# One transformer block on one core: the SBUF addresses of the MLP's matmul operands, and of one attention buffer, are moved by 64 or 192 bytes

## The chip, the cores and the metric

The kernel runs on one core of a Trainium2 chip. The metric is the device time of one execution in microseconds (us); lower is better. Three runs of the kernel before took 735.03, 736.0 and 736.13 us, median 736.0. A fourth execution was profiled: 735.27 us, of which the profile's span covers 733.4 us.

## The reference

A PixArt-style block: self-attention, cross-attention to a context, and an MLP, for 16 batches of 256 tokens with 256 features, 16 heads, and an MLP of 1024 hidden features, all in float32.

```python
x_norm = modulate(_ln(x), shift_a, scale_a)
q, k, v = jnp.split(x_norm @ W_qkv + b_qkv, 3, axis=-1)
...
x = x + gate_a[:, None] * (attn_out @ W_proj + b_proj)
q_c = _ln(x) @ W_qc + b_qc
k_c, v_c = jnp.split(_ln(context) @ W_kvc + b_kvc, 2, axis=-1)
...
x = x + (c_attn_out @ W_cproj + b_cproj)
x_norm2 = modulate(_ln(x), shift_m, scale_m)
h = jax.nn.gelu(x_norm2 @ W_mlp1 + b_mlp1)
x = x + gate_m[:, None] * (h @ W_mlp2 + b_mlp2)
```

## The kernel before

**Number format.** A matrix product is made of three float32r matmuls: each operand is split into a high part and a low part, and high·high, high·low and low·high are added in PSUM (`mm3` at L461 and `mm3_tok` at L470). The names carry it: `hh` and `hl` are the high and low parts of the hidden values, `xTh` and `xTl` those of a transposed input, `h_q` and `l_q` those of a query.

**A matmul and its operands.** Each matmul has stationary weights (128 columns, read by a weight load, `PEld` in the profile) and moving rows (256 columns, streamed by the matmul itself, `PE`). The weight load of the next matmul runs while the rows of the present one are streamed. Every 128x128x256 matmul of this kernel has a weight load of its own.

**Attention, the first 550 us.** There are 32 units (16 of self-, 16 of cross-attention). Unit n holds its queries and keys in `big[n % 3]` (L85), three buffers of 16 KB in each partition, and its values in `vts[n % 3]`. In each beat of a unit PE makes scores `s` of the next unit (for the row maxima) and transposed scores `st` of this one, both with weights and moving rows from a `big` buffer. The exponentials go to `pt` tiles (4 KB, five buffers, `exp` at L782), which are the moving rows of `o` (`av_part`, L805), four column groups of 32 with weights from `vts`. Between them stand projections of other units, with 64 rows each, in two halves of the array side by side. Their weights and rows come from `wself`, `wcross` (the resident weight tiles) and `xTh`/`xTl`.

**MLP, from 553 us on.** The 16 batches are cut in 4 chunks of 256 hidden features, 64 chunks in all. Each chunk has a first product of 12 matmuls (`mlp_first`, L920; weights `W1` = `wself`, moving rows the normalised input, which stands in the no longer used `wcross`; its PSUM tile is `ph`), a gelu on ACT (`mlp_gelu`, L953) that writes `hf` and `hh`, a subtraction on POOL that writes `hl`, and a second product of 12 matmuls (`mlp_second`, L974; weights `hh` and `hl`, moving rows `W2` = `big[2]`; PSUM tile `st` or `s`). The loop at L1274 puts the first product of chunk i+2 ahead of the second product of chunk i-1, so that PE alternates: 12 matmuls `ph`, 12 matmuls `st` or `s`, and so on. The first six batches have their input transposed by four PE transposes (`mlp_T`, L869, PSUM tile `psT_m`, moving rows `ident`); the others by DVE and DMA.

**Order and places.** Every engine's order is the program's order (`InOrder`, L40; all its instructions have line L51 in the profile). Tiles get their SBUF address in the order in which they and their tags first appear, so one tile's size moves all that follow. The kernel before already has one such shift: `ROWS` (L133) puts the MLP's input 48 elements (192 bytes) into a slot of `wcross`.

```python
ROWS = [cross(1 - i, 48) for i in range(2)]
homes = (("pt", 5), ("qkh", 3), ("qkl", 3))
W2 = [big[2][:, 0], big[2][:, 1]]
```

**Places within 256 bytes.** The built program gives each tile's byte address in its partition. Its remainder by 256 is, before: `wself` and `wcross` 32; `ROWS` 224; `big` 160, all three; `vts` 160; `hh`, `hl` and the other tiles of the tags `qkh` and `qkl` 224; `pt` 224; `xTh`, `xTl`, `xn`, `A`, `oT` 224; `ident` 128. The `homes` are the tags of `hf`, `hh` and `hl`. A matmul's slices start at multiples of 512 bytes in these tiles, except for `vts`, whose heads lie 128 bytes apart (160 and 32 in turn).

Of the kernel before, what the change touches and what calls it, by code (L numbers as in the profile page):

```python
# [10 lines left out]
F32 = mybir.dt.float32  # L11
F32R = mybir.dt.float32r
# [4 lines left out]
P = 128  # L17
# [4 lines left out]
def pixart_block(  # L22
# [8 lines left out]
    B, N, H = x.shape  # L31
# [3 lines left out]
    NT = N // P  # L35
# [24 lines left out]
    const = ctx.enter_context(tc.tile_pool(name="const", bufs=1))  # L60
    work = ctx.enter_context(tc.tile_pool(name="work", bufs=2))
# [20 lines left out]
    mhalf = const.tile([P, 2], F32, name="mhalf")  # L82
    POOL.memset(mhalf, -0.5)

    big = [const.tile([P, 2, 8, N], F32R, name=f"big{i}") for i in range(3)]  # L85
    vts = [const.tile([P, NT, NH, 32], F32, name=f"v{i}") for i in range(3)]
    mxs = [const.tile([P, 160], F32, name=f"mx{i}") for i in range(3)]
    for t_ in mxs:
# [5 lines left out]

    BMOD, BQKV, BKVC, BM1 = 0, 12, 20, 24
    BQ, BK, BQC, BKC = 32, 34, 36, 38
    ct_ = work.tile([B, 2, H], F32, tag="qkh", name="c_sb", bufs=3)
    c_sb, th = ct_[:, 0], ct_[:, 1]
    SP.dma_start(c_sb, cond)
    X = {}  # L100

# [66 lines left out]

    ts = [work.tile([P, 2, KC, H], F32, tag="pt", name=f"wf{i}", bufs=5) for i in range(3)]
    wm0, wm1, wk, wq, wv = (ts[i // 2][:, i % 2] for i in range(5))  # L170
    dummy = const.tile([P, 2], F32, name="dummy")

    def f_load():
        X[0] = work.tile([P, NT, H], F32, tag="x", name="x_0", bufs=5)
# [152 lines left out]
    def layernorm(src, name):  # L327

        o = Box()

        def stats():
            o.st = work.tile([P, NT, 6], F32, tag="bnst", name=f"st_{name}")
            for t in range(NT):
                DVE.bn_stats(o.st[:, t], src()[:, t])

        def rstd(power=True):
            o.mv = work.tile([P, NT, 2], F32, tag="bnmv", name=f"mv_{name}")
            for t in range(NT):
                DVE.bn_aggr(o.mv[:, t], o.st[:, t])
            o.rs = work.tile([P, NT], F32, tag="rstd", name=f"rs_{name}")  # L340
            if power:
                o.pow()

        def pow():
            POOL.tensor_scalar(o.rs, o.mv[:, :, 1], EPS, None, ALU.add)
            POOL.tensor_tensor(o.rs, o.rs, mhalf, ALU.pow)

        def apply(eng=E_['LN'].get(name[0])):
            o.xn = work.tile([P, NT, H], F32, tag="xn", name=f"xn_{name}", bufs=3)
            for t in range(NT):  # L350
                if eng == "act":
                    ACT.activation(o.xn[:, t], src()[:, t], AF.Identity, bias=o.nb[:, t:t + 1],
                                   scale=o.rs[:, t:t + 1])
                else:
                    (DVE if eng == "dve" else POOL).tensor_scalar(
                        o.xn[:, t], src()[:, t], o.mv[:, t, 0:1], o.rs[:, t:t + 1],
                        ALU.subtract, ALU.mult)

        def shift():
            o.nb = work.tile([P, NT], F32, tag="nb", name=f"nb_{name}")  # L360
            POOL.tensor_scalar(o.nb, o.mv[:, :, 0], -1.0, None, ALU.mult)
            POOL.tensor_tensor(o.nb, o.nb, o.rs, ALU.mult)

        o.steps, o.pow, o.shift = [stats, rstd, apply], pow, shift
        return o

# [672 lines left out]
    for n, v in (("0", u0), ("1", u1), ("2", u2)):  # L1039
        for c in "KQV":  # L1040
            o = getattr(v, c)
# [8 lines left out]
    for n, v in (("0", u0), ("1", u1), ("2", u2)):  # L1050
        word["T" + n + "t"], word["T" + n + "h"], word["T" + n + "l"] = v.T[0].parts
        word["T" + n + "p"] = v.T[0].low_pool
        for c in "KQ":
            o = getattr(v, c)
# [206 lines left out]
    last, o, q = units[-1], units[-1].post, units[-2].post  # L1261
# [97 lines left out]
```

## Time and profile before

| | |
|---|---|
| three runs | 735.03, 736.0, 736.13 us, median 736.0 |
| the profiled execution | 735.27 us, its span 733.4 us |
| busy in the span | PE 99%, PEld 87%, DVE 79%, ACT 76%, POOL 74% |
| TensorE clock granted | 1.00 in nearly all of the span |
| DMA | 35.7% of 16 engines on SP's queue |

The profile lists for each engine how long its instructions ran. PE and PEld are two records of one engine: the matmuls, and the weight loads that overlap them. Matmuls overlap each other too, since one is recorded until its last row has left the array, so the distance between the starts of two matmuls says more of the pace than their durations. The timeline view joins equal neighbours into one row: start of the first, time in which they ran, name, and their count after an x. In the `x12` rows the distance to the start of the row behind is the time of 12 matmuls.

### The profile page before, as it was taken

What the parts mean: (1) busy time and instruction counts of PE and PEld (TensorE: products, weight loads), DVE (VectorE), ACT (ScalarE), POOL (GpSimd) and SP (SyncE); (2) the same over time, 40 slices, a digit from 0 to 9 for tenths busy, and PEclk for the clock granted to TensorE, in tenths of its full rate; (3) what the DMA queues carried; (4) which work ended last, traced back from release to release, by engine and by line L of the source; (5) the groups of instructions that cost most, each with busy time, mean ns of one, the idle gap of its engine ahead of it and who ended that gap; (6) DMA issues with size and microseconds to landing.
All of it is one profiled execution on the core that took longest, in us unless ns stands there. A gap on an engine that the chain in (4) does not pass through costs nothing.

```text
span 733.4 us, 24916 instructions
## 1 busy us (share of the span) xinstructions
PE 725.7 (99%) x10112; PEld 640.9 (87%) x10112; DVE 582.1 (79%) x1218; ACT 556.2 (76%) x961; POOL 545.7 (74%) x574
## 2 busy tenths in 40 slices
PE   9999999999999999999999999999999999999997
PEld 9788888888888888888888888888888999999997
DVE  4878888889888888988888989888745676686772
ACT  4368898888888888888888888899886666666653
POOL 6877578869687786968678898889646767767743
PEclk9999999999999999999999999999999999999999
DMA  6654434433434343343434344344221313334321
GB/s 191 208 163 144 146 121 132 145 109 114 155 127 144 127 151 121 116 147 126 152 120 159 126 161 146 139 148 147 81 60 44 117 59 101 89 98 103 85 62 57
DMA packets 67109, 90.56 MB, mean 123 GB/s; under 512 B 6194, under 2 KB 38740, under 8 KB 66996
## 3 DMA queue, kind: packets, MB, share of 16 engines
q1 hardware_dynamic: 66164, 86.88, 35.7%
q8 instruction: 80, 1.31, 0.7%
q0 software_dynamic: 560, 1.84, 0.7%
q14 instruction: 33, 0.27, 0.1%
q10 hardware_dynamic: 272, 0.26, 0.1%
HBM read 26.97 MB, written 8.46 MB: 48 GB/s over the span
## 4 chain that ended last, share of the span: by engine, by line
PE 95%; DVE 2%; POOL 1%; issue 1%; ACT 1%; POOLq 0%; ACTq 0%
PE s L51 19%; PE o L51 16%; PE st L51 16%; PE ph L51 10%; PE ps_q L51 4%; PE ps_qc L51 4%; PE ps_kc L51 4%; PE ps_v_c L51 3%; PE ps_k L51 3%; PE ps_v_s L51 3%; PE ps_P_s L51 3%; PE ps_P_c L51 2%; PE ps_h L51 1%; PE psT_q L51 1%; PE psA_c L51 1%; PE psA_s L51 1%
## 5 line engine op out<-in xcount | busy, mean ns | idle before, releaser
L51 DVE TENSOR_REDUCE mx<-s 128x2 f32<-128x512 f32 x504 | 324.5, 684 | 64.1 <-PE s L51 57.0
L51 ACT ACTIVATE pt<-st 128x1024 f32<-128x1024 f32 x252 | 259.1, 1028 | 17.6 <-PE st L51 10.6
L51 PE MATMUL s<-big 63*128 63x256 f32 (+1 forms) x1024 | 186.2, 299 | 0.5 <-DVE mx L51 0.2
L51 PEld LDWEIGHTS s<-big 63*128 63x128 f32 (+1 forms) x1024 | 133.5, 186 | 19.9 <-DVE l_kc L51 6.6
L51 PE MATMUL st<-big 64*128 64x256 f32 (+1 forms) x1024 | 134.1, 297 | 0.0
L51 POOL TENSOR_TENSOR hl<-hf,hh 128x512 fp32r<-128x512 f32 x64 | 85.4, 1338 | 53.7 <-ACT hh L51 53.4
L51 PE MATMUL o<-pt,v 128*32 128x256 f32 x2048 | 123.8, 382 | 0.0
L51 PEld LDWEIGHTS st<-big 64*128 64x128 f32 (+1 forms) x1024 | 96.5, 186 | 14.6 <-issue 12.8
L51 PEld LDWEIGHTS o<-pt,v 128*32 128x32 f32 x2048 | 60.0, 109 | 41.5
L51 PE MATMUL ph<-wcross,wself 128*128 128x256 f32 x672 | 88.1, 281 | 0.0
L51 PEld LDWEIGHTS ph<-wcross,wself 128*128 128x128 f32 x672 | 82.8, 189 | 0.0
L51 ACT ACTIVATE hf<-ph,bT 128x256 f32<-128x256 f32 x114 | 48.0, 473 | 32.6 <-PE ph L51 32.6
L51 ACT ACTIVATE hh<-ph,bT 128x256 fp32r<-128x256 f32 x114 | 47.9, 472 | 25.9 <-PE s L51 13.5
L51 ACT COPY oT<-o 128x512 f32<-128x512 f32 x63 | 37.0, 587 | 33.0 <-PE o L51 33.0
L51 PE MATMUL ps_kc<-xTh_c,wcross 64*128 64x256 f32 x256 | 46.7, 292 | 0.0
L51 PE MATMUL st<-big,hh 128*128 128x256 f32 x256 | 45.8, 279 | 0.0
L51 PE MATMUL s<-big,hh 128*128 128x256 f32 x256 | 45.7, 278 | 0.0
L51 PE MATMUL ps_v_c<-wcross,xTh_c 64*128 64x256 f32 x256 | 44.2, 292 | 0.0
L51 PE MATMUL ps_k<-xTh_s,wself 64*128 64x256 f32 (+1 forms) x232 | 43.6, 294 | 0.0
L51 PE MATMUL ps_qc<-xTh_q,wcross 64*128 64x256 f32 x256 | 41.5, 282 | 0.0
L51 PE MATMUL ps_q<-xTh_s,wself 64*128 64x256 f32 (+1 forms) x240 | 40.7, 287 | 0.0
L51 POOL TENSOR_SCALAR xn_c<-c,mv_c,rs_c 128x256 f32<-128x256 f32 x32 | 39.0, 1228 | 1.7
(236 smaller groups left out, 2154.8 us busy)
## 6 DMA issues: line engine op xcount, KB each, us to landing
big<-h_kc SPq DMA_DIRECT2D x32, 256.0 KB
big<-h_qc SPq DMA_DIRECT2D x32, 256.0 KB
big<-h_k SPq DMA_DIRECT2D x30, 256.0 KB
big<-h_q SPq DMA_DIRECT2D x29, 256.0 KB
g<-gd SPq DMA_DIRECT2D x16, 256.0 KB
c<-in_ctx_dram SPq DMA_DIRECT2D x16, 256.0 KB
big<-l_kc SPq DMA_DIRECT2D x16, 256.0 KB
big<-l_qc SPq DMA_DIRECT2D x16, 256.0 KB
```

The source lines that it names most:

```text
L51: i = f(*a, **k)
```

## The change

Nothing is computed otherwise, and no instruction is added, removed or moved: on all five engines the instructions of the two built programs stand in the same order, with the same shapes and as many waits. (Two read or write `th` in a buffer of its own, which was the second half of `c_sb`.) What differs is where tiles lie. `big[2]` becomes 256 bytes larger and its view starts 64 bytes in. The tag `qkl` is first used early (by `th`), so its buffers now lie behind those of `qkh`. `dummy` grows from 8 to 96 bytes, which moves all behind it, and the tag `bnst` has five small buffers in place of two, which brings the tiles behind it back to their old remainder.

```diff
-    big = [const.tile([P, 2, 8, N], F32R, name=f"big{i}") for i in range(3)]
+    big = [const.tile([P, 16 * N + 64 * (i // 2)], F32R, name=f"big{i}") for i in range(3)]
+    big = [t[:, 16 * (i // 2):16 * (i // 2) + 16 * N].rearrange("p (a k n) -> p a k n", a=2, k=8)
+           for i, t in enumerate(big)]
...
-    ct_ = work.tile([B, 2, H], F32, tag="qkh", name="c_sb", bufs=3)
-    c_sb, th = ct_[:, 0], ct_[:, 1]
+    c_sb, th = [work.tile([B, 2, H], F32, tag=t, name=n, bufs=3)[:, 0] for t, n in (("qkh", "c_sb"), ("qkl", "th"))]
...
-    dummy = const.tile([P, 2], F32, name="dummy")
+    dummy = const.tile([P, 24], F32, name="dummy")[:, :2]
...
-            o.st = work.tile([P, NT, 6], F32, tag="bnst", name=f"st_{name}")
+            o.st = work.tile([P, NT, 6], F32, tag="bnst", name=f"st_{name}", bufs=5)
```

Call the **step** from one matmul to the next the address of the first one's moving rows less that of the next one's weights, by remainder of 256. By the built programs:

| tile | remainder before | now |
|---|---|---|
| `big[2]` (`W2`; queries and keys of every third unit) | 160 | 224 |
| `hh`, `hl` (tags `qkh`, `qkl`) | 224 | 32 |
| `pt` | 224 | 32 |
| `wself`, `wcross`, `ROWS`, `big[0]`, `big[1]`, `vts`, `xTh`, `xTl`, `xn`, `A`, `oT`, `ident` | as above | unchanged |

| from matmul to matmul | step before | now |
|---|---|---|
| within 12 `ph` | 192 | 192 |
| within 12 `st` or `s` of the MLP | 192 | 192 (0 in one run, whose `hh` and `hl` lie in `xTh` and `xTl`) |
| from `ph` to `st` or `s` of the MLP | 0 | 192 |
| from `st` or `s` of the MLP to `ph` | 128 | 192 |
| from the transposes `psT_m` to `ph` | 96 | 96 |
| within `s` or `st` of attention | 0 | 0 |
| between `s` and `st` of two units, one of them in `big[2]` | 0 | 64 or 192 |
| within `o` | 64 and 192 | 128 and 0 |

## The prediction

> **What bounds the kernel now.** I read the busy shares and the chain of waits first, then busy time by stage. The first columns of the stage rows are the stretch, its length, and PE's busy time with its matmuls.
>
> ```profile
> PE 725.7 (99%) x10112; PEld 640.9 (87%) x10112; DVE 582.1 (79%) x1218; ACT 556.2 (76%) x961; POOL 545.7 (74%) x574
> PE 95%; DVE 2%; POOL 1%; issue 1%; ACT 1%; POOLq 0%; ACTq 0%
> 200.00:360.00 160.00, 159.91 (x2632) 135.82 (x2628) 139.31 (x299) 135.22 (x210) 121.70 (x130) 1.00 0.38 135
> 660.00:724.00 64.00, 64.00 (x552) 64.00 (x551) 41.85 (x77) 38.42 (x93) 40.12 (x36) 1.00 0.31 80
> ```
>
> The chain that ended last is PE for 95%. In the MLP's stretch from 660 to 724 us PE is busy all the time, while DVE, ACT and POOL work 42, 38 and 40 us of 64. So in the MLP the end is set by how close one matmul follows another, and this can change only by PE itself: 64.00 us over 552 matmuls are 116 ns each.
>
> The timeline of PE shows that this 116 ns is a mean over two paces.
>
> ```profile
> 711.09 1.57 PE L51 MATMUL ph<-wcross,wself 128*128 128x256 f32 x12
> 712.50 0.40 PE L51 MATMUL st<-big,hh 128*128 128x256 f32 x2
> 712.75 0.28 PE L51 MATMUL st<-big,hl 128*128 128x256 f32 x1
> 712.86 0.39 PE L51 MATMUL st<-big,hh 128*128 128x256 f32 x2
> 713.09 0.28 PE L51 MATMUL st<-big,hl 128*128 128x256 f32 x1
> 713.20 0.39 PE L51 MATMUL st<-big,hh 128*128 128x256 f32 x2
> ...
> 713.89 1.57 PE L51 MATMUL ph<-wcross,wself 128*128 128x256 f32 x12
> 715.30 0.40 PE L51 MATMUL st<-big,hh 128*128 128x256 f32 x2
> ...
> 716.68 1.57 PE L51 MATMUL ph<-wcross,wself 128*128 128x256 f32 x12
> ```
>
> Twelve `ph` take 712.50 - 711.09 = 1.41 us, 117.5 ns each. The second product begins slowly (its first three matmuls take 712.86 - 712.50 = 0.36 us, 120 ns each) and then runs at 713.20 - 712.86 = 0.34 us for three, 113.3 ns each. Two pairs of runs, 48 matmuls, take 716.68 - 711.09 = 5.59 us. At the last four second products, which stand behind each other with no `ph` between them, the fast pace lasts:
>
> ```profile
> 725.05 0.39 PE L51 MATMUL s<-big,hh 128*128 128x256 f32 x2
> ...
> 728.79 0.39 PE L51 MATMUL s<-big,hh 128*128 128x256 f32 x2
> ```
>
> These are 33 matmuls in 3.74 us, 113.3 ns each, across two boundaries of runs with step 192.
>
> The pace does not belong to `ph` as such. Behind four transposes `ph` runs fast, and then the second product is the slow one:
>
> ```profile
> 583.89 0.60 PE L51 MATMUL psT_m<-ident,xn_m 128*128 128x128 f32 x4
> 584.25 1.62 PE L51 MATMUL ph<-wcross,wself 128*128 128x256 f32 x12
> 585.70 0.40 PE L51 MATMUL st<-big,hh 128*128 128x256 f32 x2
> 585.94 0.28 PE L51 MATMUL st<-big,hl 128*128 128x256 f32 x1
> 586.06 0.40 PE L51 MATMUL st<-big,hh 128*128 128x256 f32 x2
> ...
> 587.12 1.58 PE L51 MATMUL ph<-wcross,wself 128*128 128x256 f32 x12
> 596.46 0.37 PE L51 MATMUL ph<-wcross,wself 128*128 128x256 f32 x1
> L51 PE MATMUL ph<-wcross,wself 128*128 128x256 f32 x12 | 1.6, 284 | 0.0
> L51 PE MATMUL ph<-wcross,wself 128*128 128x256 f32 x24 | 3.0, 281 | 0.0
> L51 PE MATMUL s<-big,hh 128*128 128x256 f32 x25 | 4.4, 276 | 0.0
> ```
>
> The last three rows group matmuls by shape in short stretches, with mean ns of one: the `ph` of 584 us, the 24 `ph` of 580 us, and the second products of 725 us. The first `ph` behind transposes takes 0.37 us (row of 596.46), so the other eleven of 584 us take (12 x 284 - 370) / 11 = 276 ns, as the fast `s` do, against 281 ns in the 24 of 580 us. The same instructions with the same step of 192 thus run in either pace, and what went before decides. The second product of 585.70 takes 1.42 us, 118 ns each, and does not recover. Where a run stands behind another with a step of 192, the pace is kept. Where the step differs (0 into the second product, 128 into `ph`), the pace changes or stays slow: fast `ph` to slow `st` (0), slow `ph` to fast `st` within three matmuls (0), fast `st` to slow `ph` (128). I read this as two paces of the overlap between streaming rows and loading the next weights, which a steady step keeps and another step upsets.
>
> **The change part by part.**
>
> *The MLP behind the last transposes.* From 596.46 to 725.05 us lie 46 pairs of runs, 1104 matmuls, in 128.59 us. With a step of 192 throughout, and `ph` starting fast behind the transposes (their step, 96, is unchanged), they take 1104 x 113.3 ns = 125.1 us and 0.1 us for the first: 125.2, a gain of **3.4 us**. Bounds: all of it, or the slow pace throughout (117.5 ns, 129.7 us), a loss of 1.1. Nothing else would hold PE up:
>
> ```profile
> POOL hl L51 <- ACT hh L51: 41.4, 36, 1.6
> ACT hf L51 <- PE ph L51: 27.7, 44, 0.6
> ```
>
> In this stretch ACT waits for PE and POOL for ACT, and PE waits for nobody once the transposes are done; a pair that shrinks from 2.80 to 2.72 us leaves ACT (38.42 us in 64, 60%) idle time enough.
>
> *The MLP ahead of them.* From 574 to 595.5 us there are 15 runs, some fast already. By the same count they would gain 0.5 us. The transposes at 595.51 wait for DVE, whose input comes by POOL and ACT from PE:
>
> ```profile
> PE psT_m L51 <- DVE xn_m L51: 1.8, 3, 0.9
> ```
>
> Three such waits, 1.8 us, can swallow a part: I take **-0.4**, bounds -0.5 and +0.3 (slow pace throughout). From 553 to 573 us one run of 12 now has step 0, and others gain; at most 0.4 and at worst +0.2: **-0.1**.
>
> *Attention, `s` and `st`.* In each half of the array some 165 of the steps between an `s` and an `st` leave 0, and some 70 steps beside projections become 0, where one neighbour lies in `big[2]`. The page's groups give matmuls of 64 rows by step (0 for `s` and `st`, 192 for `ps_kc`, 64 for `ps_v_c`):
>
> ```profile
> L51 PE MATMUL s<-big 63*128 63x256 f32 (+1 forms) x1024 | 186.2, 299 | 0.5 <-DVE mx L51 0.2
> L51 PE MATMUL st<-big 64*128 64x256 f32 (+1 forms) x1024 | 134.1, 297 | 0.0
> L51 PE MATMUL ps_kc<-xTh_c,wcross 64*128 64x256 f32 x256 | 46.7, 292 | 0.0
> L51 PE MATMUL ps_v_c<-wcross,xTh_c 64*128 64x256 f32 x256 | 44.2, 292 | 0.0
> ```
>
> Step 0 is the slowest, by 5 to 7 ns. (165 - 70) x 5 ns = 0.5 us, the halves running side by side; part of it goes into waits of `s` on DVE's maxima. **-0.2**, bounds ±1.5 (all 300 changed steps at 5 ns).
>
> *Attention, `o`.* Its steps go from 64 and 192 to 128 and 0. Its weight loads have 32 columns:
>
> ```profile
> L51 PEld LDWEIGHTS o<-pt,v x2048: 106/110/110, 46.2 to 551.7; 128*32 128x32 f32 x187
> L51 PE MATMUL o<-pt,v x2048: 379/379/404, 46.2 to 551.9; 128*32 128x256 f32 x187
> 118.39 1.93 PE L51 MATMUL o<-pt,v 128*32 128x256 f32 x32
> ```
>
> Minimum, median and maximum hardly differ over two steps, and the eight groups of four take 1.93 us, 0.24 us each: a load of 110 ns ends well ahead of the next group. **0**, upper bound 448 groups (64 blocks of seven) x 8 ns, the excess of a slow start of the second product (120 against 113 ns), 3.6 us.
>
> *The rest.* `th` apart from `c_sb` and five `bnst` buffers change no wait on PE: **0**, hidden behind PE's 99%; without that cover a few tenths of a us of DVE's statistics.
>
> Sum, on the profiled execution: 735.27 - 3.4 - 0.4 - 0.1 - 0.2 = 731.2 us. That execution lies 0.7 below the median of the runs and 0.3 below the mean of all four (735.6), so I expect 731.5 us.
>
> **The rivals.**
>
> *Slow for good.* The slow pace is kept by a steady step as well: the 24 `ph` of 580 us stay at 281 ns. Before, the step of 0 heals it once in each pair; the change removes that. If one late wait or the boundary itself upsets the pace behind 596 us, nothing brings it back before the end: 1.1 us lost there, 0.3 ahead, and a few matmuls of entry; 735.6 + 1.5 = 737.1, up to 738. It decides once more than three quarters of the tail is slow. Against it: fast starts behind transposes, and two boundaries crossed at 725 us.
>
> *Half.* Only the entries of the second product are healed and `ph` stays slow, because its own weights, not the step, set its pace: about 0.02 us for each of 46 pairs and some at 574 us, 734.5. The fast `ph` of 584 us speaks against it.
>
> *`o` pays.* Step 0 in half of `o` costs the bound of 3.6 us: 735.1, no change. Its flat durations speak against it.
>
> *Addresses do not matter.* The two paces come from something else, such as PSUM banks: 735.6, no change. The Trainium skill says so in effect: SBUF — State Buffer, "SBUF: two separate sides", gives PE a second, independent read port for weights, and says that PE never waits for another on the engine side. By that rule nothing here changes. The trace disagrees in that equal instructions take 276 or 281 ns, but no run here has moved an address yet.
>
> **How the numbers follow.** Forecast 0.65; half 0.10; slow for good 0.13; `o` or attention pays 0.08; addresses do not matter 0.04. The likeliest time is 731.5, its own range 730.3 to 733 (attention's ±1.5 one way, and stretches that fall slow). The range for 8 in 10 reaches to half and to no change: 730.0 to 736.3; what it leaves out is slow for good, and an attention that gains its bound. A measurement of this kernel tells about 0.2% (1.5 us) from no change: faster is below 734.5. Of half, a half counts as faster, and so do a few of the attention cases: 0.65 + 0.05 + 0.02 = 0.72 faster; 0.16 the same; 0.12 slower.
>
> **What would show it.** In the profile after, 12 `ph` should take 1.36 us in place of 1.41, mean 276 ns in place of 281, and the second product 1.36 from its first matmul on; 660 to 724 us should hold 565 matmuls in place of 552. `o` should keep 379 ns and 1.93 us a block, and the attention's end (now at 552 us) should not move by more than 1.5 us. A tail with 281 ns in both products would show the first rival; 281 for `ph` alone, half; an `o` block above 1.95 us, the third rival. I am wrong if `ph` at an unchanged 1.41 us stands beside boundaries of step 192.

## The result, and the profile after

| | before | after |
|---|---|---|
| median of six runs each, us | 735.51 (733.53 to 736.13) | 741.98 (741.22 to 743.24) |
| profiled execution, us | 735.27 | 742.12 |
| its span, us | 733.4 | 740.3 |

The ratio is 1.0097, with a 95% interval of 1.0079 to 1.0114. The change makes the kernel about 1% slower, where 731.5 us was forecast. Beside the later runs the kernel before was executed 64 times more: 53 times it took 733.7 to 736.8 us, ten times 739.1 to 742.8 and once 750.5, and since no trace shows a longer one, it is open whether what is described below happens in them too.

The page of the kernel after has these busy shares, and these shares of the chain of waits:

```profile
PE 726.7 (98%) x10112; PEld 638.9 (86%) x10112; DVE 591.1 (80%) x1218; ACT 555.7 (75%) x961; POOL 547.4 (74%) x574
PE 84%; DVE 8%; POOL 2%; DMA 2%; SPq 1%; issue 1%; ACT 1%; DVEq 0%; POOLq 0%; ACTq 0%
```

Before, PE was 95% of the chain and DVE 2%. Now DVE has 8%, and the DMA and SP's queue 3% together. The stage from 660 to 724 us shows it (stretch, its length, busy time of PE, PEld, DVE, ACT and POOL with instruction counts):

```profile
660.00:724.00 64.00, 61.21 (x518) 59.39 (x517) 48.72 (x82) 36.11 (x87) 39.88 (x34) 1.00 0.29 84
```

From 660 to 724 us PE starts 518 matmuls where 552 stood before and 565 were forecast, and it is idle there for 2.8 us, where it was never idle before. The 47 that are missing against the forecast amount to 5.3 us at 113 ns, so the idle time in the records shows only a part of the waiting. The time of one matmul is not what got longer. PE's timeline of the kernel after shows the first product of each batch's first chunk (the row with one `ph` apart, or the longer x12 row), and the runs around one of them:

```profile
613.06 1.76 PE L51 MATMUL ph<-wcross,wself 128*128 128x256 f32 x12
...
625.31 0.35 PE L51 MATMUL ph<-wcross,wself 128*128 128x256 f32 x1 [0.97 <-DVE wcross L51]
...
664.57 1.52 PE L51 MATMUL ph<-wcross,wself 128*128 128x256 f32 x12
665.92 0.39 PE L51 MATMUL s<-big,hh 128*128 128x256 f32 x2
...
667.28 1.52 PE L51 MATMUL ph<-wcross,wself 128*128 128x256 f32 x12
...
673.35 0.35 PE L51 MATMUL ph<-wcross,wself 128*128 128x256 f32 x1 [0.46 <-DVE wcross L51]
673.98 1.54 PE L51 MATMUL ph<-wcross,wself 128*128 128x256 f32 x11 [0.28 <-DVE wcross L51]
...
720.75 1.86 PE L51 MATMUL ph<-wcross,wself 128*128 128x256 f32 x12
```

Between the waits the change does what it was forecast to do. Twelve `ph` take 665.92 - 664.57 = 1.35 us, twelve `s` 667.28 - 665.92 = 1.36 us, 113 ns a matmul in both. But at the first `ph` of each batch PE waits, nearly always for its input, `wcross` (the slot `ROWS`, written by DVE). From 613.06 to 720.75 us lie nine batches of four pairs: 107.69 us, 11.97 us a batch. Before, the same two instructions stood at 713.89 us (its row is in the prediction) and at 613.33:

```profile
613.33 1.57 PE L51 MATMUL ph<-wcross,wself 128*128 128x256 f32 x12
```

That is 100.56 us, 11.17 a batch. The difference, 7.1 us in nine batches, less the 0.27 us that the kernel after was ahead at 613 us, is the 6.9 us by which the span grew.

### The profile page after: what moved, and what is told of

It is laid out like the page before. It is cut to its first block, busy times and chain, and to the rows that moved or that the text cites. A ratio compares the mean times of both kernels' runs of the same rounds, so it can differ in the third digit from the quotient of the medians.

```text
span 740.3 us, 24916 instructions
## 1 busy us (share of the span) xinstructions
PE 726.7 (98%) x10112; PEld 638.9 (86%) x10112; DVE 591.1 (80%) x1218; ACT 555.7 (75%) x961; POOL 547.4 (74%) x574
## 4 chain that ended last, share of the span: by engine, by line
PE 84%; DVE 8%; POOL 2%; DMA 2%; SPq 1%; issue 1%; ACT 1%; DVEq 0%; POOLq 0%; ACTq 0%
PE s L51 16%; PE o L51 16%; PE st L51 13%; PE ph L51 5%; PE ps_q L51 4%; PE ps_qc L51 4%; PE ps_kc L51 4%; PE ps_v_c L51 3%; PE ps_P_s L51 3%; PE ps_k L51 3%; PE ps_v_s L51 3%; DVE xn_m L51 2%; DVE wcross L51 2%; PE ps_P_c L51 2%; DMA yT<-z 2%; DVE z L51 2%
## 5 line engine op out<-in xcount | busy, mean ns | idle before, releaser
L51 POOL TENSOR_TENSOR hl<-hf,hh 128x512 fp32r<-128x512 f32 x64 | 87.6, 1372 | 47.7 <-ACT hh L51 47.5
```

What stands on the lines that cost most here:

```text
L51: i = f(*a, **k)
```

## Who makes the input late

The views of waits from 600 to 722 us (who waited <- for whom: us in total, times, longest) give, first of the kernel before and then of the kernel after:

```profile
DVE z L51 <- DMA yT<-z: 17.5, 10, 3.2
```

```profile
DVE z L51 <- DMA yT<-z: 27.3, 10, 4.0
PE ph L51 <- DVE wcross L51: 4.3, 11, 1.0
```

The chain of waits of the kernel after shows the way round that these rows are part of (start us, us, what):

```profile
675.62 1.63 DVE xn_m L51 x2
677.26 1.08 DVE z L51 x2
...
678.36 0.55 SPq L51
...
680.40 2.17 DMA yT<-z
...
682.71 0.75 DVE z L51 x2
...
683.54 1.33 DVE wcross L51
...
684.90 0.69 DVE wcross L51
685.59 0.68 DVE mt L51 x2
...
686.29 1.48 DVE y L51
687.78 1.63 DVE xn_m L51 x2
```

This is a **circle**, once per batch. DVE normalises batch b+2 (`xn_m`) and transposes it into `z`; SP issues the four transfers to `yT` (`mlp_turn`); DVE waits for them, scales `yT` into `z`, and splits it into `wcross` for PE (`mlp_turned`, a cast and a subtraction); then come the residual of the batch that is done (`mt`, `y`) and the next `xn_m`, behind all this in DVE's order. One round takes 687.78 - 675.62 = 12.16 us here. By the program's waits PE stands in it nowhere, except that `mt` reads its sums. So a faster PE need not shorten it.

The rounds can be read from DVE's `z` behind the transfers. The first and the tenth of these in the kernel before, and then in the kernel after:

```profile
610.03 0.74 DVE L51 TENSOR_SCALAR z<-yT,sc,cpT 128x256 f32<-128x256 f32 x2 [2.79 <-DMA yT<-z]
...
708.85 0.74 DVE L51 TENSOR_SCALAR z<-yT,sc,cpT 128x256 f32<-128x256 f32 x2 [3.23 <-DMA yT<-z]
```

```profile
610.15 0.74 DVE L51 TENSOR_SCALAR z<-yT,sc,cpT 128x256 f32<-128x256 f32 x2 [2.81 <-DMA yT<-z]
...
718.05 0.74 DVE L51 TENSOR_SCALAR z<-yT,sc,cpT 128x256 f32<-128x256 f32 x2 [3.74 <-DMA yT<-z]
```

Before, a round took 98.82 / 9 = 10.98 us in the mean, a little less than PE's 11.17 for a batch. That is not the length that the circle has by itself: its first rounds are uneven (10.09, 11.85 and 9.79 us), and then DVE keeps step with PE, as its `xn_m` show best:

```profile
646.88 0.73 DVE L51 TENSOR_SCALAR xn_m<-x,mv_m,rs_m 128x256 f32<-128x256 f32 x2
...
702.75 0.73 DVE L51 TENSOR_SCALAR xn_m<-x,mv_m,rs_m 128x256 f32<-128x256 f32 x2
```

These are five rounds in 55.87 us, 11.17 each, with the input ready 1.2 to 2.2 us ahead of PE all along. After, a round takes 107.90 / 9 = 11.99 us, and PE's batch, cut to 4 x 2.72 = 10.88, waits for it. So the circle kept up before and sets the pace now, although no instruction of DVE changed. Where it grew is shown by DVE's instructions from 600 to 722 us, grouped by shape (the last numbers are the busy time, the mean ns of one, and idle time before them), before and after:

```profile
L51 DVE TENSOR_SCALAR xn_m<-x,mv_m,rs_m 128x256 f32<-128x256 f32 x20 | 8.3, 455 | 0.0
L51 DVE TENSOR_TENSOR wcross<-z,wcross 128x512 fp32r<-128x512 f32 x10 | 6.9, 692 | 0.3
```

```profile
L51 DVE TENSOR_SCALAR xn_m<-x,mv_m,rs_m 128x256 f32<-128x256 f32 x20 | 17.1, 894 | 0.0
L51 DVE TENSOR_TENSOR wcross<-z,wcross 128x512 fp32r<-128x512 f32 x10 | 9.0, 899 | 0.3
```

Two `xn_m` take twice 0.44 us more and a subtraction 0.2, 1.1 us a round, of which a shorter `y` gives back 0.16 and a shorter cast 0.10: 0.8 us in all, as much as from 11.17 to 11.97. The timeline of the kernel after shows POOL beside a slow `xn_m`:

```profile
663.47 1.74 POOL L51 TENSOR_TENSOR x<-x,cb 128x512 f32<-128x512 f32 x1
...
663.99 1.71 DVE L51 TENSOR_SCALAR xn_m<-x,mv_m,rs_m 128x256 f32<-128x256 f32 x2
```

POOL's addition of the bias (`mlp_bias`) started 0.52 us ahead of `xn_m`, and the two `xn_m` took 1.71 us. Before, `xn_m` ran at 658.06 and the addition at 660.33 us, apart from each other, and the two took 0.72 us:

```profile
658.06 0.72 DVE L51 TENSOR_SCALAR xn_m<-x,mv_m,rs_m 128x256 f32<-128x256 f32 x2
...
660.33 1.75 POOL L51 TENSOR_TENSOR x<-x,cb 128x512 f32<-128x512 f32 x1
```

The first late input can be followed to a small shift between two starts. Before, DVE's subtraction began 0.26 us ahead of POOL's `hl`; after, it began 0.05 us behind it:

```profile
611.33 0.69 DVE L51 TENSOR_TENSOR wcross<-z,wcross 128x512 fp32r<-128x512 f32 x1
...
611.59 1.58 POOL L51 TENSOR_TENSOR hl<-hf,hh 128x512 fp32r<-128x512 f32 x1 [1.50 <-ACT hh L51]
```

```profile
611.40 1.29 POOL L51 TENSOR_TENSOR hl<-hf,hh 128x512 fp32r<-128x512 f32 x1 [1.43 <-ACT hh L51]
611.45 1.79 DVE L51 TENSOR_TENSOR wcross<-z,wcross 128x512 fp32r<-128x512 f32 x1
```

Whichever starts later takes longer: POOL 1.58 us in the kernel before, against 1.29 when it is first; DVE 1.79 us in the kernel after, against 0.69. POOL came 0.19 us earlier because its input comes by ACT from a faster PE, and DVE came 0.12 us later. DVE's subtraction then ended at 613.24, after PE's first `ph` of the batch had started at 613.06. That one reads the high part, the next ones read the low part that the subtraction writes, and they waited: these 12 matmuls took 1.76 us in place of 1.52. The Trainium skill describes such a thing: by SBUF — State Buffer, "SBUF: two separate sides", VectorE and GpSimd share a pair of ports as "an exclusive lock, not a bandwidth split", which the one that starts first keeps for its whole instruction. These four rows agree with it: the later one ends 1.15 us (POOL) and 0.55 us (DVE) behind the end of the first, a little less than the 1.29 and 0.69 us that it takes when it is first.

At this point the theory was: (1) the addresses make PE faster as forecast; (2) the circle takes over as the bound; (3) it is longer than before because POOL, which follows PE, now works beside DVE. The expectations call this theory A. The rivals were that the moved addresses themselves slow DVE's instructions (theory B), that ACT or POOL holds PE up and not the circle (theory C), and that the circle had almost no room before, so that anything that makes DVE a little later must cost as much (in the last expectation this is theory A, and its opposite theory D).

## The experiments

The times of the kernel before beside these runs had medians of 735.28 to 735.61 us. The ratios, with 95% intervals, are taken over all executions but the one of 750.5 us, and not from the medians.

**1 and 2. The circle's DVE work earlier.** In the kernel after (e1) and in the kernel before (e2), normalising and turning batch b+2 moves from the second chunk of a batch to the first, right behind `mlp_turned`:

```diff
             (mlp_turned if by_dma[0] else mlp_T)(b + 1)
+        if c == 0 and by_dma[1]:
+            mlp_apply(by_dma[1])
+            mlp_turn(by_dma[1])
         if c == 0 and by_dma[2]:
             mlp_load(by_dma[2])
...
         if c == 1:
-            if by_dma[1]:
-                mlp_apply(by_dma[1])
-                mlp_turn(by_dma[1])
```

> The changed kernel, with DVE's normalisation and transposes of batch b+2 moved ahead of the two multiplications and the addition that close batch b-1 (two lines of the loop). Theory A (a loop over DVE, SP's queue and DMA, some 11.9 us a batch, has taken over from PE, whose own work is now 10.9 us a batch): the loop loses about 2.3 us a batch, PE no longer waits for the split input, and the fast pace shows in the time: 732 us, 3.5 below the kernel before. Theory B (the moved addresses themselves make DVE and POOL slower): DVE's normalisation stays at 0.9 us and the time stays above 738.

> The kernel before, with the same two lines moved. Theory A: PE sets its tail already (11.2 us a batch), so nothing is won: 735.5, within 0.7 us of the kernel before. Theory B says nothing of it; a gain of over 1.5 us would mean that the move helps by itself and that e1 proves less.

Measured: 764.85 us (1.0411, 1.0382 to 1.0441) and 763.77 us (1.0383, 1.0368 to 1.0399). Both expectations were missed by about 30 us. The waits of e1 from 600 to 722 us:

```profile
POOL x L51 <- DMA x<-x2d: 44.3, 7, 8.1
DVE st_m L51 <- POOL x L51: 41.9, 8, 6.2
```

SP issues its transfers in the program's order. The load of `x` of batch b+3 now stood behind the four `yT` transfers, which wait for DVE; so POOL's addition, DVE's statistics `st_m`, `xn_m` and the next transfers waited in turn for the load. That is a new circle, of 14.6 us a batch in e1 (seven rounds of `z` from 611.89 to 714.19 us). In e2 the same two rows have 36.6 and 42.4 us. Since the kernel before lost the same, the edit says nothing on the addresses. It shows that what sets the time here is who stands behind whom on DVE's and SP's queues.

**3. PE slowed again, with the addresses of after.** One more matmul in each first product, from the 15th chunk on, whose sum the first real matmul overwrites:

```diff
+        if b * NCH + c >= 14:
+            PE.matmul(ph[:, 0], W1[0][:, 0, 2 * c * P:(2 * c + 1) * P], M[b].xT[0][:, 0], start=True, stop=True)
```

> The changed kernel with one matmul more in each of the last 50 first products (its first matmul done twice, 113 ns each, 5.6 us of PE work in all). Theory A: PE's batch becomes 11.3 us, near what the loop can follow while its lead lasts, so PE waits less; the extra work makes the kernel faster than the changed one, about 737. Theory B, or a loop that needs 11.9 us whatever PE does: 742 or more.

Measured: 737.38 us (1.0032, 1.002 to 1.0044), 4.6 us less than the kernel after, with 50 matmuls more. First its stage from 660 to 724 us, then its `xn_m` among the groups from 600 to 722:

```profile
660.00:724.00 64.00, 64.00 (x567) 64.00 (x566) 43.12 (x77) 37.96 (x91) 39.73 (x35) 1.00 0.31 83
```

```profile
L51 DVE TENSOR_SCALAR xn_m<-x,mv_m,rs_m 128x256 f32<-128x256 f32 x20 | 7.3, 402 | 0.0
```

PE is busy throughout, at the fast pace. `xn_m` takes 402 ns at the moved addresses, against 894 in the kernel after. So theory B falls: not the address slows DVE, but what runs beside it. And a PE that needs 11.3 us for a batch in place of 10.88 ends earlier, because DVE and POOL fall back into the old order: in the timeline none of the ten `xn_m` has the addition beside it.

**4. POOL's addition one chunk later.**

```diff
         if c == 2:
             if by_pe:
                 M[by_pe].ln.pow()
-            if by_dma[2]:
-                mlp_bias(by_dma[2])
         if c == 3:
...
             if by_dma[2]:
+                mlp_bias(by_dma[2])
                 mlp_stats(by_dma[2])
```

> The changed kernel with POOL's bias addition of a later batch moved one chunk later, away from DVE's normalisation. Theory A with its second part (the loop became longer because DVE's normalisation now runs beside that addition, 0.9 us for one where it took 0.46): normalisation back to 0.46 us, a loop of about 11 us, 733 to 736. If the overlap is not what slows it: 742, normalisation at 0.9.

Measured: 742.6 us (1.0101, 1.0077 to 1.0125), a miss: nothing gained. DVE's groups from 600 to 722 us:

```profile
L51 DVE TENSOR_TENSOR wcross<-z,wcross 128x512 fp32r<-128x512 f32 x10 | 13.9, 1391 | 0.3
L51 DVE TENSOR_SCALAR xn_m<-x,mv_m,rs_m 128x256 f32<-128x256 f32 x20 | 11.2, 597 | 0.0
```

`xn_m` is shorter, 597 ns, but the subtraction takes 1391 ns in place of 899: the contention moved to another instruction of the same circle. Moving POOL's addition to this place is no remedy.

**5 and 6. The circle made shorter.** As in e1, but with the load of `x` ahead of the turn's transfers on SP's queue; with the addresses of after (e5) and of before (e6):

```diff
+        if c == 0 and by_dma[2]:
+            mlp_load(by_dma[2])
         if c == 0 and b + 1 < B:
             (mlp_turned if by_dma[0] else mlp_T)(b + 1)
-        if c == 0 and by_dma[2]:
-            mlp_load(by_dma[2])
+        if c == 0 and by_dma[1]:
+            mlp_apply(by_dma[1])
+            mlp_turn(by_dma[1])
...
         if c == 1:
-            if by_dma[1]:
-                mlp_apply(by_dma[1])
-                mlp_turn(by_dma[1])
```

> As e1, but with the load of batch b+3 on SP's queue again ahead of the four transfers of the turn (in e1 it stood behind them, and POOL's addition, DVE's statistics and the next turn waited for it in a circle of about 14 us). Theory A (the circle z - wcross - mt - y - xn - transposes - SP - DMA, 12.0 us a batch in the changed kernel, is what PE waits for): without mt and y in it the circle takes about 9.7 us, less than PE's 10.9; ph starts without waiting, the tail runs at the fast pace, 732 us. Theory C (the circle is not what holds PE; ACT or POOL would be next): 737 to 742.

> The kernel before with the lines of e5. Theory A: PE sets the pace there already, 11.2 us a batch: 735.3, within 0.7. A gain of more than 1.5 would mean that e5's gain is not the addresses'.

Measured: e5 732.17 us (0.9942, 0.9918 to 0.9967), e6 736.1 us (0.9994, 0.9966 to 1.0021). **e5 is faster than both kernels.** The same two rows of e5:

```profile
660.00:724.00 64.00, 64.00 (x567) 64.00 (x566) 40.77 (x76) 39.25 (x94) 39.89 (x36) 1.00 0.33 83
```

```profile
L51 DVE TENSOR_SCALAR xn_m<-x,mv_m,rs_m 128x256 f32<-128x256 f32 x20 | 15.1, 794 | 0.0
```

PE is busy throughout with 567 matmuls, where 565 were forecast. `xn_m` still takes 794 ns, now beside an `hl`: the contention is there, but it costs nothing now, since the transfers are under way early and the input lies ready 2.5 to 4 us ahead of PE (from the end of the subtraction to the first `ph` of its batch, in the timelines). In e6 the same order of instructions gains nothing, since there PE alone is the bound. The difference between e5 and e6 is the addresses alone: 3.9 us between the medians, and 3.0 us between the means of the executions with a granted clock of 0.998. In the two traces, from the first `ph` behind the last transposes to the start of the last matmul, PE takes 129.19 and 132.55 us, 3.4 us less.

**7. The four transfers on two queues**, in the kernel after:

```diff
-            SP.dma_start(m.y[:, a].rearrange("p k c -> p (k c)"),
+            (SP, ACT)[a % 2].dma_start(m.y[:, a].rearrange("p k c -> p (k c)"),
```

> The changed kernel, with two of the four transfers of each turn issued by ACT instead of SP, so that the last one is issued 1.2 us earlier. Theory A: the circle gets shorter by up to 1.2 us a batch, some 10.8 us, and the time falls to 732 to 736, unless ACT, which waits for DVE's transposes in order, is held up with its gelus. Theory C: no gain, 742.

Measured: 740.76 us (1.0048, 1.0012 to 1.0084), scattered from 736.22 to 744.21; the profiled execution was the slowest, 744.21. The input was ready 1.7 to 4.4 us early, so the circle was no longer the bound. But ACT's queue now held transfers that wait for DVE (ACT stood idle for 5.26 and 4.95 us around those of 605.62 and 620.43 us), and early in the tail, the MLP behind the last transposes, PE waited for ACT (from 600 to 640 us):

```profile
PEld ph L51 <- ACT hh L51: 5.4, 2, 3.2
```

After the second of these waits, which ended at 623.57 us, PE fell into the slow pace. It kept that to the end, at a granted clock of 1.00:

```profile
660.00:724.00 64.00, 64.00 (x545) 64.00 (x545) 50.64 (x84) 36.93 (x91) 45.53 (x38) 1.00 0.33 86
```

These are 117.4 ns a matmul: the prediction's rival "slow for good", in a run that forced a stall, and shown for this one execution.

**8. POOL's addition left out**, in the kernel after:

```diff
-            if by_dma[2]:
-                mlp_bias(by_dma[2])
```

> The changed kernel without POOL's bias addition for the last ten batches (their MLP input lacks that bias; 1.7 us of POOL and nothing else left out). Theory A, second part (in the changed kernel DVE's normalisation runs beside that addition and takes 0.89 us in place of 0.46, which lengthens the circle from 11.0 to 12.0 us a batch): normalisation back to 0.46 or less, circle about 11.0, next to PE's 10.9: 733 to 735. If the circle needs 12 us for another reason: 740 or more.

Measured: 732.01 us (0.9931, 0.9894 to 0.9969). DVE's groups from 600 to 722 us:

```profile
L51 DVE TENSOR_SCALAR xn_m<-x,mv_m,rs_m 128x256 f32<-128x256 f32 x20 | 8.3, 456 | 0.0
L51 DVE TENSOR_TENSOR wcross<-z,wcross 128x512 fp32r<-128x512 f32 x10 | 6.9, 693 | 0.3
```

Ten instructions of POOL (the one shown above took 1.74 us) are worth 10 us on PE's path. Without them `xn_m` and the subtraction take the times of before, and PE runs at 10.88 us a batch and waits for nobody from 600 to 722 us. DVE keeps step with it: a round takes 10.7 us in the mean, and 10.88 in the last four (from `xn_m` at 657.10 to 700.63 us). This is the most direct test of (3), and it shows that a circle with the instruction times of before can follow the faster PE.

**9. Is there room in the kernel before?** Two small writes on DVE, 0.37 us in all, into buffers no longer used, ahead of `mlp_apply`:

```diff
             if by_dma[1]:
+                DVE.memset(mxs[0], 0.0)
+                DVE.memset(mxs[1], 0.0)
                 mlp_apply(by_dma[1])
```

> The kernel before with two small memsets on DVE ahead of each normalisation of the last ten batches, some 0.45 us a batch that nobody waits for otherwise. Theory A (in the kernel before the circle has 11.0 us a batch against PE's 11.2, and the split input is 1.2 to 2.2 us ahead of ph): the circle becomes 11.4, the lead is used up within some five batches and PE waits behind it: 738 to 741. Theory D (the circle had room before, and only the new addresses or the new phases made it long): no change, 735.4.

Measured: 735.44 us (0.9968, 0.9933 to 1.0004), no loss; theory A falls. A round still took 10.99 us in the mean, and PE waited for nobody, since other instructions of the round grew shorter:

```profile
L51 DVE TENSOR_SCALAR xn_m<-x,mv_m,rs_m 128x256 f32<-128x256 f32 x20 | 6.6, 369 | 0.0
```

(455 ns before; the cast took 518 ns in place of 891, and `y` 1215 in place of 1364.) So the circle's length isn't a fixed sum of its instructions. It depends on which of POOL's instructions each of them meets, and 0.37 us more on DVE did not upset the order of before.

## Why the prediction was wrong, point by point

**The MLP's two paces: right.** A step of 192 throughout gives 113 ns a matmul in both products, from the first one on, and e5 against e6 prices the tail at 3.4 us, as forecast. The rivals "half" and "addresses do not matter" fall with that: with nothing but addresses moved, two products take 2.72 us in place of 2.79. So what the prediction drew from the Trainium skill (SBUF — State Buffer, "SBUF: two separate sides"), that nothing would change, is not what was measured. Why the addresses matter, and which of the moved tiles counts, no run shows: all were moved at once.

**The term ahead of 596 us: mis-sized.** Forecast -0.4. PE reached the transposes of 583.9 us 0.27 us earlier (583.62) and waited 0.34 us there, where it had not waited before. It reached those of 595 us at 595.52 us (before 595.51), waited 0.53 us there in place of 0.38, and began the tail 0.16 us later than before. These waits on `xn_m` swallowed all of the gain and not a part.

**Attention: right, within its bounds.** The upper bound for `o` was counted too high (an excess of 120 - 113 = 7 ns in 448 groups is 3.1 us, not 3.6), which changes nothing here. `o` keeps its durations (minimum, median and maximum), a block of it its 1.93 us, and its last matmul starts at 551.8 us in place of 551.9:

```profile
L51 PE MATMUL o<-pt,v x2048: 378/379/404, 46.1 to 551.8; 128*32 128x256 f32 x187
```

**"Nothing else would hold PE up": the step that failed.** It was argued from ACT and POOL waiting for PE, from idle shares, and from PE waiting for nobody. In the kernel after, PE waits 4.3 us for `wcross`, and a batch takes 11.97 us where 10.88 was forecast. What the argument left out is DVE: its `z` waits 17.5 us in ten rounds for `yT`, a row of the same view that the prediction does not take up. Followed round, it gives the circle, and a rival "DVE's circle becomes the bound" was thus to be had from the trace. Its price was not to be had from the length of a round. Before, a round keeps step with PE and so tells only that the circle keeps up; and in e8, with the instruction times of before and without POOL's additions, it follows PE at 10.88 as well. The forecast took it that the other engines' instructions keep their times. It needed the thought that POOL follows PE by way of ACT, while DVE's waits tie it to PE hardly at all, so that a faster PE can shift the two against each other and make DVE's instructions longer.

**Slow for good: wrong here, but real.** It was given as the way to lose, and the loss came by another. Its mechanism does occur. In the kernel after, the wait at 649.87 us is followed by seven slow runs, up to the next wait at 661 us (the first two `ph` of these in PE's timeline):

```profile
652.68 1.58 PE L51 MATMUL ph<-wcross,wself 128*128 128x256 f32 x12
655.51 1.58 PE L51 MATMUL ph<-wcross,wself 128*128 128x256 f32 x12
```

From one to the next are two runs, 2.83 us, 118 ns a matmul, with step 192: 84 matmuls x 4 ns, 0.3 us. In e7 it took the whole tail.

**What stays open.** Why a round settles at 12 us and doesn't slip back; e3 shows that a batch of 11.3 us on PE does lead back. The timelines give a hint: of the twenty pairs of `xn_m` that the two kernels have from 600 to 722 us, nineteen start 0.46 to 0.48 us behind the end of an `hl` of POOL, and in the kernel after, from 627 to 700 us, it is an `hl` that the addition follows at once. That would tie the circle to POOL and, by ACT, to PE; no run tests it. How much more room than 0.37 us the kernel before had wasn't tried. And why a wait starts the slow pace at one place (649.87 us) and not at others (673.98 us).

## What to carry to other kernels

Before speeding up the engine that is busy all the time, look in the same stage for closed circles among the others (here DVE, SP's queue and a DMA) and measure a round against one round of the bound. A round that keeps step with the bound tells only that it keeps up, and not how much shorter it could be; nor is the lead of the input over its reader (here 1.2 to 2.2 us) a reserve to count on, if instructions of the circle can get longer. Engines that follow the sped-up one move against those that don't, and where two of them hold each other up, the same instructions can get longer. If a circle is close, shorten it together with the change: the same addresses cost 6.5 us alone, and with the turn and the load issued earlier they bring the kernel below both.

## What the runs showed of the hardware

- Where the operands lie in SBUF changes the pace of back-to-back 128x128x256 matmuls with a weight load each: 113 ns or 117.5, at a granted clock of 1.00. With a step of 192 throughout, either pace is kept; a wait can start the slow one. Only this one set of places was tried, so the step, a remainder of 256, is a way to describe it and not a tested rule.
- Where an instruction of DVE and one of POOL overlapped, the one that began later took longer (four rows at 611 us). A shift of 0.31 us between two starts, from 0.26 us ahead to 0.05 us behind, made DVE's subtraction 1.1 us longer.
- One more matmul per chunk made the kernel after 4.6 us faster, and ten additions on POOL cost 10 us of the whole, since both change who meets whom.
